# An attention and mixture-of-experts block: unfilled expert slots are skipped, weight tiles serve early reads, and TensorE's results join a partial sum

## The chip, the cores and the metric

The kernel runs on one core of one Trainium2 chip. The metric is the time of one execution on the device in microseconds. Before the change the median of six runs is 1692.75 us (1690.46 to 1701.3).

The core has five engines with a queue of instructions each: TensorE (PE, matrix multiplication; its weight loads are listed as PEld), VectorE (DVE), ScalarE (ACT), GpSimd (POOL) and SyncE (SP, which issues transfers here). Each works through its own queue in order and waits for the others through semaphores. The transfers (DMA) of all queues run on the same 16 DMA engines.

## The reference

T = 4096 tokens (16 sequences of 256) of width 256, in float32:

```python
x = x + layernorm(attention(layernorm(x)))     # 16 heads of 128, weights = codes * scales
h = layernorm(x)
scores = softmax(h @ gate.T)                   # 64 experts in 8 groups, the best 3 groups count
topk_w, topk_i = top 6 experts of each token
pos  = how many earlier (token, k) pairs chose the same expert
slot = expert * 96 + min(pos, 95)              # 96 slots an expert
buf[slot] = h[token]                           # a later token overwrites slot 95
out  = (silu(buf @ Wg.T) * (buf @ Wu.T)) @ Wd.T            # per expert, 96 rows
y    = sum over k of topk_w * out[slot]
x = x + layernorm(y + shared(h))               # shared: one gated layer of width 352
```

Most pairs of a crowded expert land in its last slot, so many tokens share that one row. An expert that few tokens chose leaves slots unfilled.

## The kernel before, in words

Three parts follow each other.

**Attention and routing (0 to about 1320 us).** A loop over 16 sequences x 16 heads runs as a software pipeline (project, scores, transpose, weigh; one head a step). A scheduler orders all queues but SP's first loads; the program can pin an instruction behind another on its engine (`issue_after`). Two sequences at a time, `route` finds the experts of 512 tokens and scatters their rows (token row, token number, weights) into `buf_d` with 24 indirect transfers on POOL (L584). In between, `check_codes` loads the weight codes again, piece by piece, and ORs their bits on DVE (L612), to see whether the codes fit the shorter format that this run assumes. `clear_slots` and `clear_sums` fill `buf_d` with a row that says "unfilled" (token number T + slot) and the sums with zero.

**Experts (about 1397 to 1588 us).** From here on the order of every queue is that of the program (`manual_schedule`). Experts come in groups of four. In the turn of expert e, PE transposes the rows of e + 2 (`bp`), multiplies those of e by Wg and Wu (`pg`), transposes the product of e - 1 (`ap`) and multiplies that of e - 2 by Wd (`eo`). ACT scales the result (`ob`), and POOL adds the 96 rows with an indirect, accumulating transfer (L885) to one of three sums in DRAM, `y0` to `y2`, at the rows' tokens. The sums take turns, so that neighbouring scatters don't wait for each other; `y2` takes none from expert 44 on. Rows of unfilled slots and of the last slots go to rows T to T + 95. The last slots' rows go into `ol` as well (L892, a transfer on ACT's queue, one a group); they reach their many tokens by a matmul later. Five groups of weights (`wg`, `wu`, `wd`, three tiles a group) are in SBUF; the next group's are loaded in the second turn of each group, after the next rows (`bn`, L828), all from SP. While the experts run, PE also computes pieces of the shared layer.

**Closing (about 1588 us to the end).** The output is made in eight chunks of 512 tokens, in the order `ends`: 0 to 3 (shared part already in y0), SG0 = 4 (shared part in SBUF, `ss`), and G = 5, G + 1, G + 2, whose shared part PE adds here. `pieces` says which parts of the shared layer PE computes between them (`shared_in`, followed by Silu on ACT and a product `aT` on DVE, `shared_act`). For chunk n the program issues: `put_out` (PE: last slots by `ovT` and `ol`, and the shared part, into a PSUM tile `ov`, of which there are two), the add of `ov` to the chunk's sum (DVE, L984), the statistics (DVE L991 and L992, ACT L994), the sum of the next chunk (`sum_y`: POOL y0 + y1, L969; DVE + y2, L970), and the normalization of chunk n (`norm_out`: DVE L1001 and L1003, ACT L1005, POOL + x L1006, output by SP L1007). y0, y1, y2 and `ovT` are loaded into tiles that take the place of the weights (L957, L959, L904).

Of the kernel before, what the change touches and what calls it, by code (L numbers as in the profile page):

```python
# [9 lines left out]
F32 = mybir.dt.float32  # L10
# [8 lines left out]
P = 128  # L19
# [31 lines left out]
def block_kernel(ctx, tc, x, wq, sq, wk, sk, wv, sv, wo, so, bqk, bv, bo, gateT, wg, wu, wd, sgT, suT, sdT, out):  # L51
# [10 lines left out]
    y_ds = [dram.tile([T + CAP, D], F32, name=f"y{i}_d") for i in range(NY)]  # L62
# [26 lines left out]
    def attention(split):  # L89
# [151 lines left out]
        def clear_sums(i):  # L241
            with tc.issue_after(marks[-1].ins):
                nc.vector.memset(zero, 0.0)
            r0 = 0 if i else SG0 * CG * P
            n = (T - r0) // P
            nc.sync.dma_start(
                y_ds[i][r0:T].rearrange("(p r) d -> p r d", p=P), zero.unsqueeze(1).to_broadcast([P, n, D])
            )
            nc.sync.dma_start(y_ds[i][T : T + CAP], zero[0:CAP, 0:D])
# [358 lines left out]
        def check_codes(n):  # L608

            todo = [(nm, j, i) for nm in views for j in range(NPC) for i in range(2)]  # L610
            if chks:
                nc.vector.tensor_tensor(bits, bits, chks.pop(), ALU.bitwise_or)  # L612
# [87 lines left out]
    def ffn(nm_, last_route, ph0):  # L700
# [72 lines left out]

        def load_group(g):
            w_g = ewp.tile([P, EG, DC, M], F32, tag="wg", name=f"wg{g}")
            nc.sync.dma_start(w_g, wg[:, g * EG : (g + 1) * EG])
            w_u = ewp.tile([P, EG, DC, M], F32, tag="wu", name=f"wu{g}")
            nc.sync.dma_start(w_u, wu[:, g * EG : (g + 1) * EG])
            w_d = ewp.tile([MH, EG, 2, D], F32, tag="wd", name=f"wd{g}")
            nc.sync.dma_start(w_d, wd[:, g * EG : (g + 1) * EG])  # L780
            wts[g] = (w_g, w_u, w_d)
# [94 lines left out]
        def expert_out(e):  # L876
# [5 lines left out]
            for mc in range(2):  # L882
# [6 lines left out]
                bounds_check=T + CAP - 1, oob_is_err=True, compute_op=ALU.add,  # L889
# [6 lines left out]
        ends = [0, G, 1, G + 1, 2, G + 2, 3, SG0]  # L896
        pieces = {0: [(G + 1, 1)], 1: [(G + 1, 2)], 2: [(G + 2, 0), (G + 2, 1)], 3: [(G + 2, 2)]}
        y2s = {}

        def load_y2(g):  # L900

            t = xp.tile([P, EG * RW], F32, tag="bn", name=f"y2_{g}", bufs=5)
            y2s[g] = t[:, 0 : CG * D].rearrange("p (c d) -> p c d", d=D)
            nc.sync.dma_start(y2s[g], y_ds[2][g * CG * P : (g + 1) * CG * P].rearrange("(c p) d -> p c d", p=P))  # L904

        with tc.manual_schedule():
# [7 lines left out]
            for e in range(E + 2):  # L914
# [11 lines left out]
                if e < E:  # L926
                    expert_mul(e, sg, pg)
                else:
                    if e > E:
                        shared_act(G, 0)  # L930
# [10 lines left out]
                if j == 1 and g >= 1:  # L941
                    if g + 3 < NG_:
                        load_buf(g + 3)
                    if g + EWB - 1 < NG_:
                        load_group(g + EWB - 1)
                    if g + 3 > NG_ and g < NG_:
                        load_y2(ends[g + 2 - NG_])

            ph3.close()
            yp = ph2.enter_context(tc.tile_pool(name="yp" + nm_, bufs=8, reuse_waits="tile"))  # L950
            loaded, stat = {}, {}

            def load_y(g):
                r = slice(g * CG * P, (g + 1) * CG * P)
                ys = [yp.tile([P, CG, D], F32, tag=f"y{i}", name=f"y{i}_{g}") for i in range(2)]
                for i in range(2):
                    nc.sync.dma_start(ys[i], y_ds[i][r].rearrange("(c p) d -> p c d", p=P))  # L957
                ovT = yp.tile([E, CG * P], F32, tag="ovT", name=f"ovT{g}")
                nc.sync.dma_start(ovT, ovT_d[:, r])  # L959
                if g not in y2s:  # L960
                    load_y2(g)
                loaded[g] = ovT, ys

            def sum_y(g, parts):

                ys = loaded[g][1]
                for c, n in parts:
                    r = slice(c, c + n)
                    nc.gpsimd.tensor_add(ys[0][:, r, :], ys[0][:, r, :], ys[1][:, r, :])  # L969
                    nc.vector.tensor_add(ys[0][:, r, :], ys[0][:, r, :], y2s[g][:, r, :])  # L970
                    if g == SG0:
                        nc.vector.tensor_add(ys[0][:, r, :], ys[0][:, r, :], ss[g][:, r, :])

            def put_out(g, c):

                ovT, y = loaded[g][0], loaded[g][1][0]
                po = ps.tile([P, 2, D], F32, tag="o", name=f"ov{g}_{c}")
                for i in range(2):
                    if g > SG0:
                        shared_out(po[:, i, :], g, c + i, True, False)  # L980
                    nc.tensor.matmul(  # L981
                        po[:, i, :], lhsT=ovT[:, (c + i) * P : (c + i + 1) * P], rhs=ol, start=g <= SG0, stop=True
                    )
                return lambda: nc.vector.tensor_tensor(y[:, c : c + 2, :], y[:, c : c + 2, :], po, ALU.add)  # L984

            def take_stats(g, c0, n):

                st = yp.tile([P, n, 6], F32, tag=f"st{n}", name=f"st{g}_{c0}", bufs=2)
                mv = yp.tile([P, n, 2], F32, tag=f"mv{n}", name=f"mv{g}_{c0}", bufs=2)
                for i in range(n):  # L990
                    nc.vector.bn_stats(st[:, i, :], loaded[g][1][0][:, c0 + i, :])  # L991
                    nc.vector.bn_aggr(mv[:, i, :], st[:, i, :])  # L992
                rs = yp.tile([P, n], F32, tag=f"rs{n}", name=f"rs{g}_{c0}", bufs=2)
                nc.scalar.activation(rs, mv[:, :, 1], AF.Sqrt, bias=eps_t)  # L994
                stat[g, c0] = rs, mv

            def norm_out(g, c0, n, eng):

                y = loaded[g][1][0][:, c0 : c0 + n, :]
                rs, mv = stat.pop((g, c0))  # L1000
                nc.vector.reciprocal(rs, rs)  # L1001
                nb = yp.tile([P, n], F32, tag=f"nb{n}", name=f"nb{g}_{c0}", bufs=2)
# [3 lines left out]
                eng.tensor_add(y, y, xs[:, g * CG + c0 : g * CG + c0 + n, :])  # L1006
                nc.sync.dma_start(out_v[:, g * CG + c0 : g * CG + c0 + n, :], y)  # L1007

            whole, halves = [(0, CG)], [(0, 2), (2, 2)]
            for g in ends[0:5]:  # L1010
                load_y(g)
# [5 lines left out]
            sum_y(ends[0], whole)  # L1017
            for n, g in enumerate(ends):
                last = n == len(ends) - 1
                nx = ends[n + 1] if not last else None  # L1020
                add = [put_out(g, 0), put_out(g, 2)]
                if n == 0:
                    shared_act(G + 1, 0)
                for u in pieces.get(n, []):
                    shared_in(*u)
                if last:
                    add[0]()
                    take_stats(g, 0, 2)
                    norm_out(g, 0, 2, nc.gpsimd)
                    add[1]()  # L1030
                    take_stats(g, 2, 2)
                    norm_out(g, 2, 2, nc.vector)
                    continue
                for f in add:
                    f()
                for u in pieces.get(n - 1, []):
                    shared_act(*u)
                take_stats(g, 0, CG)
                if n + 5 < len(ends):
                    load_y(ends[n + 5])  # L1040
                sum_y(nx, halves if n + 2 == len(ends) else whole)
                norm_out(g, 0, CG, nc.gpsimd)
            ph4.close()
            ph2.close()
# [48 lines left out]
```

## Time and profile before

| | |
|---|---|
| median of six runs | 1692.75 us |
| profiled execution | 1692.43 us |
| its span, first to last instruction | 1690.6 us |
| attention and routing, to 1320 us | PE busy 1142.9, DVE 961.9 us |
| rest of routing, first shared pieces, 1320 to 1397 | PE busy 71.9 of 77 us |
| experts, 1397 to 1588 | PE busy 183.1 of 191 us, DMA share 0.76 |
| closing, 1588 to 1690.6 | PE busy 68.6, DVE 47.8, POOL 36.8 of 102.6 us |

The profile is of one execution. "Busy" is time in which an engine ran an instruction. Idle time of an engine costs only where the end of the kernel waits for it, so it is read together with the chain of waits: followed back from the last instruction, at each step to what released it. A queue's name with a q (SPq, ACTq) means the issue of transfers. L12 is line 12 of the kernel.

### The profile page before, as it was taken

Reading aid. Unit: us, or ns where it says so; the run is one execution under the profiler, and the core shown is the slowest. Engines: PE = TensorE matmul, PEld = TensorE weight load, DVE = VectorE, ACT = ScalarE, POOL = GpSimd, SP = SyncE. Lnnn points to the kernel's source line nnn. Section 1 sums busy time; section 2 is a strip of 40 time slices with the busy share of each in tenths; the row PEclk is TensorE's granted clock in tenths of the full one; section 3 lists DMA queues with packets and bytes.
Section 4 is the critical chain, followed back from the end, with each engine's and each line's share of the span. In section 5 each row is a group of like instructions: output and inputs, shape, how many; then the busy total and the mean of one; then the engine's idle time right before and its main releaser. Section 6 shows DMA issues by size and latency. Waiting matters only on the chain.

```text
span 1690.6 us, 24626 instructions
## 1 busy us (share of the span) xinstructions
PE 1466.5 (87%) x8476; PEld 1237.7 (73%) x8476; DVE 1109.6 (66%) x3477; ACT 669.9 (40%) x1798; POOL 364.8 (22%) x333
## 2 busy tenths in 40 slices
PE   7999999599869968994999499959858999989894
PEld 5788898589768957894889498948757658868542
DVE  5879898488648855984798379838837614434344
ACT  4645554254335423542454245424424423223252
POOL 2410002300310040005000500140233034444443
PEclk9999999799979988998999799969979999999895
DMA  5364313410000000000000000000001676887781
GB/s 160 111 180 128 106 66 99 140 45 26 26 4 26 2 15 1 26 1 11 1 26 1 9 1 26 2 6 13 19 25 36 202 208 188 240 237 181 149 251 54
DMA packets 87175, 128.82 MB, mean 76 GB/s; under 512 B 12742, under 2 KB 69638, under 8 KB 85632
## 3 DMA queue, kind: packets, MB, share of 16 engines
q1 hardware_dynamic: 63024, 97.69, 19.3%
q0 software_dynamic: 18064, 17.82, 5.2%
q10 hardware_dynamic: 5952, 11.63, 2.1%
q8 instruction: 70, 1.15, 0.3%
q14 instruction: 65, 0.53, 0.1%
HBM read 81.98 MB, written 66.29 MB: 88 GB/s over the span
## 4 chain that ended last, share of the span: by engine, by line
PE 73%; another core or an unknown queue 9%; DVE 7%; DMA 3%; issue 3%; ACT 3%; POOL 1%; ACTq 0%; SPq 0%; POOLq 0%; DVEq 0%
PE po L353 12%; PE pq L308 12%; PE sc L320 11%; PE pt L342 7%; PE pp L372 6%; PE pv L293 6%; PE sp L736 4%; PE pg L857 4%; PE eo L883 3%; PE so L752 2%; PE ov L752 1%; ACT pe L328 1%; PE ov L981 1%; DMA wg<-wg 1%
## 5 line engine op out<-in xcount | busy, mean ns | idle before, releaser
L328 ACT ACTIVATE pe<-sc,nms 128x256 f32<-128x256 f32 x512 | 240.2, 475 | 217.3 <-DVE nms L324 156.1
L344 ACT COPY pT<-pt 128x512 f32<-128x512 f32 x256 | 150.3, 587 | 398.5 <-PE pt L342 251.1
L353 PE MATMUL po<-pT,v 128*128 128x256 f32 x1024 | 285.6, 392 | 17.1 <-DVE oT L357 11.6
L342 PE MATMUL pt<-ident,pe 128*128 128x128 f32 x1024 | 177.4, 285 | 141.2 <-DVE pe L334 102.7
L584 POOL DMA_INDIRECT buf_d<-h,si x192 | 189.3, 986 | 507.8 <-DVE si L581 428.7
L320 PE MATMUL sc<-qk 128*128 128x256 f32 x1024 | 274.0, 389 | 7.3 <-DVE qk L313 5.9
L342 PEld LDWEIGHTS pt<-ident,pe 128*128 128x128 f32 x1024 | 129.1, 144 | 188.1 <-issue 131.7
L313 DVE TENSOR_TENSOR qk<-pq,bqk_t 128x512 f32<-128x512 f32 x256 | 174.7, 682 | 107.0 <-remote 85.2
L308 PE MATMUL pq<-xnT,wq 128*128 128x256 f32 x1024 | 221.3, 332 | 0.6 <-DVE wq L191 0.4
L353 PEld LDWEIGHTS po<-pT,v 128*128 128x128 f32 x1024 | 181.1, 196 | 40.0 <-ACT pT L344 16.0
L355 DVE TENSOR_SCALAR oT<-po,bv_t 128x256 fp32r<-128x256 f32 x256 | 122.9, 480 | 117.4 <-PE po L353 53.4
L320 PEld LDWEIGHTS sc<-qk 128*128 128x128 f32 x1024 | 180.6, 195 | 25.8 <-DVE qk L313 5.7
L322 DVE TENSOR_REDUCE nm<-sc 128x2 f32<-128x512 f32 x256 | 175.1, 684 | 35.6 <-remote 16.9
L308 PE MATMUL pq<-xnT,wk 128*128 128x256 f32 x1024 | 177.0, 292 | 0.4 <-DVE wk L191 0.4
L308 PEld LDWEIGHTS pq<-xnT,wq 128*128 128x128 f32 x1024 | 162.3, 197 | 15.0 <-issue 1.5
L293 PE MATMUL pv<-wv,xnT 128*128 128x512 f32 x512 | 165.2, 444 | 2.7 <-POOL wv L195 2.5
L334 DVE TENSOR_SCALAR pe<-pe,rsum 128x256 f32<-128x256 f32 x512 | 164.7, 364 | 1.4
L308 PEld LDWEIGHTS pq<-xnT,wk 128*128 128x128 f32 x1024 | 146.5, 196 | 2.5 <-DVE wk L191 1.1
L372 PE MATMUL pp<-wo,oT 128*128 128x256 f32 x1024 | 136.1, 288 | 0.0
L372 PEld LDWEIGHTS pp<-wo,oT 128*128 128x128 f32 x1024 | 127.3, 191 | 1.0
L446 POOL DMA_DIRECT2D h_d<-h x9 | 7.4, 819 | 552.5 <-DVE h L441 275.6
L357 DVE SCALAR_TENSOR_TENSOR oT<-po,bv_t,oT 128x256 fp32r<-128x256 f32 x256 | 122.2, 477 | 2.7
(206 smaller groups left out, 1907.7 us busy)
## 6 DMA issues: line engine op xcount, KB each, us to landing
y<-y_d SPq DMA_DIRECT2D x24, 512.0 KB
wg<-wg SPq DMA_DIRECT2D x16, 704.0 KB
wu<-wu SPq DMA_DIRECT2D x16, 704.0 KB
wd<-wd SPq DMA_DIRECT2D x16, 704.0 KB
y_d<-zero SPq DMA_DIRECT2D x2, 4096.0 KB
buf_d<-empty SPq DMA_DIRECT2D x1, 6528.0 KB
bn<-buf_d SPq DMA_DIRECT2D x12, 408.0 KB
hs<-hT_d ACTq DMA_DIRECT2D x8, 512.0 KB
```

Source lines behind the costliest of these rows:

```text
L293: nc.tensor.matmul(pv, lhsT=x[:, dc, c * P : (c + 1) * P], rhs=ws["wv", j][:, dc, :], start=i == 0, stop=i == len(terms) - 1,)
L308: nc.tensor.matmul(pq[:, m, :], lhsT=w[:, dc, o : o + HD], rhs=x[:, dc, :], start=i == 0, stop=i == len(terms) - 1,)
L313: marks[0:] = [nc.vector.tensor_tensor(qk, pq, bqk_t[:, h, :].unsqueeze(2).to_broadcast([P, 2, S]), ALU.add)]
L320: nc.tensor.matmul(sc[:, c, :], lhsT=qk[:, 0, c * P : (c + 1) * P], rhs=qk[:, 1, :], start=True, stop=True)
L322: nc.vector.tensor_reduce(nm, sc, AX.X, ALU.max, negate=True)
L328: nc.scalar.activation(pe[:, c, :], sc[:, c, :], AF.Exp, bias=nms[:, c : c + 1], scale=SC, accum_out=ssum[:, c : c + 1])
L334: nc.vector.tensor_scalar_mul(pe[:, c, :], pe[:, c, :], rs[:, c : c + 1])
L342: nc.tensor.transpose(pt[:, kc, c * P : (c + 1) * P], pe[:, c, kc * P : (kc + 1) * P], ident)
L344: nc.scalar.copy(pT[b, h], pt)
L353: nc.tensor.matmul(po, lhsT=v[:, kc, o : o + HD], rhs=t[:, kc, :], start=kc == 0, stop=kc == 1)
L372: nc.tensor.matmul(pp, lhsT=x[:, h, c * P : (c + 1) * P], rhs=ws["wo", h // HPG][:, h % HPG, :], start=i == 0, stop=i == len(terms) - 1,)
L584: ins = nc.gpsimd.indirect_dma_start(out=buf_d[:, :], out_offset=bass.IndirectOffsetOnAxis(ap=si[:, c, k : k + 1], axis=0), in_=h[:, c, :] ...
```

## The change

1. **Unfilled rows.** `y0` to `y2` lose the 96 padding rows. A row whose number is T or more is outside the bound; the scatter now skips it in silence. The zero fill of the padding goes.
2. **Bit check.** The OR of `check_codes` is pinned behind the latest `qk` add, so that it stays in the step in which the program has it.
3. **One weight tile a group.** `wg`, `wu`, `wd` of a group are slices of one tile. A tile that has become free after the last groups is used for a chunk's y0, y1, y2 and `ovT`. `ovT` and y2 (finished at expert 41) are read in the turns 49, 53, 57, 61 and 65, where weights were loaded before; y0 and y1 after the last expert.
4. **Closing order.** `ov` is added to y2 as soon as PE has it. One step later follow y0 + y1 (POOL), + y2 (DVE) and the statistics, another step later the normalization. For chunk SG0, POOL adds the shared part to y2. SG0 and 3 swap places, and one piece of the shared layer comes a step earlier. The reads of the last three chunks wait for the output of the first three, whose tiles they get.

The core of the diff:

```diff
-    y_ds = [dram.tile([T + CAP, D], F32, name=f"y{i}_d") for i in range(NY)]
+    y_ds = [dram.tile([T, D], F32, name=f"y{i}_d") for i in range(NY)]
...
-            nc.sync.dma_start(y_ds[i][T : T + CAP], zero[0:CAP, 0:D])
...
             if chks:
-                nc.vector.tensor_tensor(bits, bits, chks.pop(), ALU.bitwise_or)
+                with tc.issue_after(marks[-1].ins):
+                    nc.vector.tensor_tensor(bits, bits, chks.pop(), ALU.bitwise_or)
...
+        def group_tile(name):
+            return ewp.tile([P, EG * (2 * DC * M + 2 * D)], F32, tag="w", name=name)
         def load_group(g):
-            w_g = ewp.tile([P, EG, DC, M], F32, tag="wg", name=f"wg{g}")
-            nc.sync.dma_start(w_g, wg[:, g * EG : (g + 1) * EG])
...
+            t = group_tile(f"w{g}")
+            n = EG * DC * M
+            w = [t[:, i * n : (i + 1) * n].rearrange("p (e c m) -> p e c m", e=EG, c=DC) for i in range(2)]
+            w.append(t[0:MH, 2 * n :].rearrange("p (e c d) -> p e c d", e=EG, c=2))
+            for a, b in zip(w, (wg, wu, wd)):
+                nc.sync.dma_start(a, b[:, g * EG : (g + 1) * EG])
...
-                bounds_check=T + CAP - 1, oob_is_err=True, compute_op=ALU.add,
+                bounds_check=T - 1, oob_is_err=False, compute_op=ALU.add,
...
-        ends = [0, G, 1, G + 1, 2, G + 2, 3, SG0]
-        pieces = {0: [(G + 1, 1)], 1: [(G + 1, 2)], 2: [(G + 2, 0), (G + 2, 1)], 3: [(G + 2, 2)]}
+        ends = [0, G, 1, G + 1, 2, G + 2, SG0, 3]
+        pieces = {0: [(G + 1, 1)], 1: [(G + 1, 2), (G + 2, 0)], 2: [(G + 2, 1)], 3: [(G + 2, 2)]}
...
+        def load_first(g):
+            t = group_tile(f"y{g}")
+            ys[g] = [t[:, i * CG * D : (i + 1) * CG * D].rearrange("p (c d) -> p c d", d=D) for i in range(NY)]
+            ovTs[g] = t[0:E, NY * CG * D : NY * CG * D + CG * P]
+            nc.sync.dma_start(ovTs[g], ovT_d[:, g * CG * P : (g + 1) * CG * P])
+            load_sum(g, 2)
...
                     if g + EWB - 1 < NG_:
                         load_group(g + EWB - 1)
-                    if g + 3 > NG_ and g < NG_:
-                        load_y2(ends[g + 2 - NG_])
+                    else:
+                        load_first(ends[g + EWB - 1 - NG_])
...
             def put_out(g, c):
-                ovT, y = loaded[g][0], loaded[g][1][0]
+                y = ys[g][2][:, c : c + 2, :]
...
+            def sum_y(g, c, n):
+                y = [t[:, c : c + n, :] for t in ys[g]]
+                nc.gpsimd.tensor_add(y[0], y[0], y[1])
+                if g == SG0:
+                    nc.gpsimd.tensor_add(y[2], y[2], ss[g][:, c : c + n, :])
+                nc.vector.tensor_add(y[0], y[0], y[2])
...
+            for i in range(n + 1):
+                if i < n:
+                    add = [put_out(ends[i], 0), put_out(ends[i], 2)]
+                    if i == 0:
+                        shared_act(G + 1, 0)
+                    for u in pieces.get(i, []):
+                        shared_in(*u)
+                    for f in add:
+                        f()
+                    for u in pieces.get(i - 1, []):
+                        shared_act(*u)
+                if i == n:
+                    break
+                if i:
+                    g = ends[i - 1]
+                    sum_y(g, 0, CG)
+                    take_stats(g, 0, CG)
+                if i > 1:
+                    norm_out(ends[i - 2], 0, CG, nc.gpsimd)
+                    if i - 2 + EWB < n:
+                        load_first(ends[i - 2 + EWB])
+                        load_rest(ends[i - 2 + EWB])
+            g = ends[-1]
+            sum_y(g, 0, 2)
+            take_stats(g, 0, 2)
+            norm_out(ends[-2], 0, CG, nc.gpsimd)
+            sum_y(g, 2, 2)
+            norm_out(g, 0, 2, nc.gpsimd)
+            take_stats(g, 2, 2)
+            norm_out(g, 2, 2, nc.vector)
```

## The prediction

> **What bounds the kernel now.** I read the page first, then the busy times by stage, the chain of waits over the expert part and the closing part, the waits of SP's queue, and the timeline of the closing part. The page and the stages:
>
> ```profile
> span 1690.6 us, 24626 instructions
> PE 1466.5 (87%) x8476; PEld 1237.7 (73%) x8476; DVE 1109.6 (66%) x3477; ACT 669.9 (40%) x1798; POOL 364.8 (22%) x333
> ```
>
> ```profile
> 1397.00:1588.00 191.00, 183.14 (x1102) 152.51 (x1101) 74.10 (x261) 54.01 (x136) 90.88 (x64) 0.98 0.76 193
> 1588.00:1690.60 102.60, 68.64 (x187) 37.69 (x185) 47.84 (x117) 34.87 (x57) 36.79 (x18) 0.75 0.60 172
> ```
>
> In a stage row the numbers are length, then busy time of PE, PEld, DVE, ACT and POOL. Up to 1588 PE is busy 183 of 191 us: only its stalls can be won there. In the closing 102.6 us no engine is full (PE 68.6, DVE 47.8, POOL 36.8): that stretch is made of waits. The chain of waits shows PE's stalls in the expert part, and SP's waits show what lies behind them:
>
> ```profile
> 1471.08 5.07 DMA wg<-wg
> ...
> 1496.21 9.06 DMA wg<-wg
> 1505.34 0.58 ACTq L892
> ```
>
> ```profile
> SPq L828 <- DMA y_d<-ob,bn: 113.5, 16, 10.9
> ```
>
> ACT issues a small transfer (`ol`, L892) once per group; it can go only when a weight load has landed, and the Silu that PE's next expert needs stands behind it in ACT's queue. The weight loads stand behind `bn` loads on SP, which wait 113.5 us in total for scatters. So late scatters make late weights make a blocked ACT: 5.07 + 9.06 = 14.1 us, and some 2 us more at half clock (the pg/eo matmuls after 1506 take about twice as long).
>
> In the closing part the timeline of all engines shows a ring:
>
> ```profile
> 1640.04 1.23 DVE L970 TENSOR_TENSOR y<-y,y 128x1024 f32<-128x1024 f32 x1
> 1641.18 0.17 DVE L1001 RECIPROCAL rs<-rs 128x4 f32<-128x4 f32 x1
> 1641.38 0.16 DVE L1003 SCALAR_TENSOR_TENSOR nb<-mv,rs 128x4 f32<-128x4 f32 x1
> ...
> 1641.58 2.08 ACT L1005 ACTIVATE y<-y,nb,rs 128x256 f32<-128x256 f32 x4 [1.14 <-DVE nb L1003]
> ...
> 1643.73 2.34 POOL L1006 TENSOR_TENSOR y<-y,xs 128x1024 f32<-128x1024 f32 x1 [7.94 <-ACT y L1005]
> ...
> 1646.03 2.34 POOL L969 TENSOR_TENSOR y<-y,y 128x1024 f32<-128x1024 f32 x1
> ...
> 1648.41 1.23 DVE L970 TENSOR_TENSOR y<-y,y 128x1024 f32<-128x1024 f32 x1
> ```
>
> POOL's queue is in program order, so its sum for a later chunk (L969) stands behind the residual add of an earlier one (L1006). That add waits for ACT's normalization, which waits for DVE's `nb`, which in DVE's queue follows the sum that waits for POOL. From start to start: sum 1.14, `rs` and `nb` 0.40, ACT 2.15, POOL 2.30 + 2.38 = 8.37 us, exactly 1640.04 to 1648.41. The statistics (L991, L992) aren't in it: here they run on DVE while ACT and POOL are at work.
>
> **The change part by part.** Times below are in the clock of this trace.
>
> Skipped rows. The reference's routing on its inputs leaves 21 of 64 experts under 96 tokens; with the last slot of each, 1146 of 6144 rows (19%) are not scattered. That a skipped row costs no packet shows in the scatter of L584: 192 instructions of 128 rows are 24576 rows, but POOL's queue has 18064 packets in all. POOL's own 1.43 us a scatter stay. The scatters of j=2 and 3 of a group sit on the loop scatter, `bn`, weights (its period is 12.6 us: `bn` at 1458.07, 1470.65, 1483.34). Of those that gate the weights behind the 9.06 us stall (experts up to 27) the empty rows make 2.8 full scatters (experts 10, 19, 22, 23); scatters follow each other at 2 to 3 us in such a burst, so SP gains about 7 us there. The deleted padding DMAs (3 x 96 KB, issued far from any wait) are worth 0.
>
> One weight tile instead of three. The load of a group now waits until the group's last `eo` has run, not its last `pg`: the first refill moves from 1405.39 to where wd goes now, 1411.81, with wu, wd and the next `bn` behind it on SP. Later ones wait for `bn` anyway. Cost to the loop: 0 to 6.4 us; I take 3. Net, SP is 4 us early at the 9 us stall, and PE leaves the expert part x = 4 us early. Bounds: -4 (no gain from rows, refill late) to +16 (all stalls go).
>
> The `bits` ORs move from 97 to 390 us to steps 88 to 216, some 430 to 1050 us: 33 x 0.68 = 22.4 us of DVE. There PE is busy 69.6 of 70 us in the even batches and DVE 57.8, so four ORs a batch (2.7 us) fit in 12 us of idle DVE: 0. If that cover is gone it is the 22.4 us. The DVE waits on their loads now (L612, 9.4 us) lie in a stretch where 16 steps take the same 70 us as without them, so nothing is won either. Range: -2 to +4.
>
> Early reads. `ovT` and y2 of four chunks now arrive during the expert part and the fifth's right after it, so PE's 5.6 us wait for `ovT` at 1592.33 goes: PE runs on. On SP they stand behind the last `bn` and weights and ahead of the y0/y1 reads, so nothing urgent is queued behind them. They add 2 x 0.64 MB and 2 x 0.13 MB to two y2 reads that are there now, each of which stretched a scatter by about 1 us: the scatters may end 2 us later, but the first y0/y1 sums aren't what is late (below). Chunks 5 to 7 get the tiles of chunks 0 to 2, so SP holds their reads until that chunk's output has been written: for chunk 5 by about 1628, with `ovT` there at 1631 and PE asking for it at 1638. Hidden by 7 us; if it is later, PE waits the rest.
>
> The closing order. Now chunk i's `ov` is added to y2, and only one step later come POOL's y0+y1, DVE's sum, the statistics of that sum; then `nb` of the chunk before. So DVE's 2.14 us of statistics (four pairs, 1602.58 to 1604.72) enter the ring between sum and `rs`: 8.37 + 2.14 = 10.5 us a chunk, whatever PE does. What is late next is that ring. Step by step, with PE free at 1592.3 - x: `ov` of an unshared chunk 1.9, of a shared one 8.3, a piece of `shared_in` 3.6 (chain rows of L981, L752, L736).
> - The sum of chunk 1 stands on DVE behind the `ov` adds of chunk 2: 1592.3 + 1.9 + 3.6 + 8.3 + 7.1 + 1.9 = 1615.1, adds and two `aT` 2.0: 1617.1. (Before: 1604.72.)
> - Sum 2 is PE's: 1.3 for a PSUM buffer, 3.6 + 8.3 of PE, 1.4 of DVE: 1629.7. Sums 3, 4, 5 by the ring: 1640.2, 1650.7, 1661.2. Sum 6 carries the shared part on POOL, 2.3 more: 1674.0. (Before, sum 6 is at 1662.92.)
> - Tail: 8.1 to POOL's first half of the last chunk, 1.3 to its sum, 6.5 through statistics, chunk 6's `nb`, ACT and POOL to the second half, then 1.3 + 1.0 + 1.0 + 0.8 + 1.1 + 0.7 to the last add: 1695.8. From the last add's end to the span's end it is now 1683.2 to 1690.6, 7.4: 1703.2 - x.
> - PE idles some 4.5 us before the last shared chunk (its `aT` waits in ACT's queue behind a normalization). In this trace 3.0 us of idle (1643.3 to 1646.3) was followed by a granted clock of 0.50 from 1646 to 1658, where 20 of these 24 matmuls and the 8 with `ol` took 14.3 us. So that chunk may take 16.6 in place of 8.3, and the end is 1708 - x.
>
> The Trainium skill, "TensorE: Matmul & The Clock Gate", Part 1, says that about 3.4 us of sustained work brings the clock back. By it the chunk would take about 10 us, the ring would stay the bound, and the slow case would fall away. This trace differs: the clock stayed at half for 12 us of unbroken matmuls.
>
> I take the middle of 1703.2 and 1708: 1705.5 - 4 = 1701.5, against 1690.6. The profiled execution took 1692.43, 1.8 more than its span and 0.3 under the median 1692.75: **1703 us**.
>
> **The rivals.**
> - Expert stalls vanish (x = 15). The completion semaphore that L892 shares with a weight load depends on the order of the DMAs, which the single tile shifts; against it, order and number in a group stay the same. 1705.5 - 15 + 1.8 = 1692: no change.
> - Faster: the ring does not hold, because sum, normalization and residual add of neighbouring chunks overlap. Then PE decides, with 52.3 us of closing work (1.9 x 5 + 8.3 x 3 + 3.6 x 5): 1644.6, plus 1.3 for the adds and 20 from the last chunk's first sum to the end, minus x: 1662, or 1664 in time. It decides from the point where a ring step is under PE's 6.5 us a chunk. Against it: the 8.37 above closes to the last digit with queues in order.
> - Rows and tiles win nothing (x = -4): 1711.
> - The ORs are exposed: 1703 + 22 = 1725. For it, only that PE is full there.
>
> **How the numbers follow.** A measurement tells about 0.3% (5 us) from no change: 1687.7 to 1697.8. Forecast 0.50, with its own range 1696 to 1710; vanishing stalls 0.20; nothing won 0.13; faster ring 0.08; exposed ORs 0.09. Faster is the faster ring and a little of the vanishing stalls, 0.11; no change is most of that rival and the forecast's low end, 0.27; slower 0.62. Leaving out the faster ring, the exposed ORs and some edge, the range is 1688 to 1712.
>
> **What would show it.** Right: L970's successor starts 10.5 us apart in the later closing steps, with statistics between sum and `nb`; the second sum near 1613; no wait for `ovT`; the last POOL sums 10 us later than now; `bn` loads under 12.6 us apart around experts 20 to 27. Wrong: ring steps of 8 us or less, POOL's sums not waiting behind L1006's add, attention's 70 us batches longer by more than 1 us, or the two expert stalls gone.

## The result and the profile after

The changed kernel takes 1704.98 us (median of 20 runs, 1699.03 to 1710.33) where the kernel before took 1693.36 in the same comparison (46 runs): ratio 1.0062, 95% interval 1.005 to 1.0074, slower by 0.6%. The forecast was 1703. The profiled execution took 1702.36 us. Its page begins:

```profile
span 1700.5 us, 24626 instructions
PE 1457.4 (86%) x8476; PEld 1233.2 (73%) x8476; DVE 1105.8 (65%) x3475; ACT 666.1 (39%) x1796; POOL 366.7 (22%) x334
```

The same stages (length, then busy time of PE, PEld, DVE, ACT, POOL, then the granted clock, the DMA share and GB/s):

```profile
1397.00:1588.00 191.00, 184.34 (x1089) 151.23 (x1088) 73.46 (x256) 53.90 (x136) 85.92 (x61) 0.98 0.76 199
1588.00:1700.50 112.50, 56.84 (x176) 32.15 (x174) 44.32 (x114) 30.65 (x53) 44.31 (x22) 0.74 0.43 134
```

PE is busy for less time in the closing stretch than before, and the stretch is longer: it is made of waits, more than before. A cleaner cut is by the Silu of the experts. The first is at 1396.6 (before 1400.7), the last at 1571.05 (1575.7). So attention and routing are 4.1 us shorter, the expert part 0.5 us, and the closing part, from the last Silu to the end of the span, grows from 114.9 to 129.5: +14.6. Together that is +9.9 us of span.

In the expert part the chain of waits (start, us, what) no longer has the two stalls of before, but others of the same make:

```profile
1484.56 13.25 DMA w<-wd
1497.88 0.61 ACTq L896
...
1512.26 12.22 DMA y_d<-ob,bn
1524.68 3.94 DMA bn<-buf_d
1528.70 0.59 ACTq L896
```

ACT's small transfer `ol` (L896 now) still waits, here until a load of weights (`wd`) and a load of rows (`bn`) have landed. In the trace each of the two loads has the completion semaphore that `ol` uses next, and ACT waits for it first. SP's wait for scatters ahead of `bn` (total, times, longest) is no shorter than the 113.5 us of before:

```profile
SPq L832 <- DMA y_d<-ob,bn: 119.6, 16, 12.8
```

The skipped rows are seen in POOL's DMA queue. First before, then after: packets, MB, share:

```profile
q0 software_dynamic: 18064, 17.82, 5.2%
```

```profile
q0 software_dynamic: 18064, 16.66, 4.8%
```

The packets are as many, only the bytes fall. In the trace 1146 packets of the experts' scatters now have 8 bytes and take 11 ns each on average, and the other 4998 have 1024 bytes and take 127 ns (125 before).

A piece of the closing ring, from the timeline of all engines (DVE sum L982, `nb` L1001; ACT square root L992, normalization L1003):

```profile
1636.18 1.22 DVE L982 TENSOR_TENSOR y<-y 128x1024 f32<-128x1024 f32 x1 [2.12 <-POOL y L979]
...
1639.75 1.28 ACT L992 ACT_TABLE_LOAD   x1 [6.41 <-DVE rs L999]
1639.76 0.16 DVE L1001 SCALAR_TENSOR_TENSOR nb<-mv,rs 128x4 f32<-128x4 f32 x1
...
1641.04 0.30 ACT L992 ACTIVATE rs<-mv,eps_t 128x4 f32<-128x4 f32 x1
1641.25 2.06 ACT L1003 ACTIVATE y<-y,nb,rs 128x256 f32<-128x256 f32 x4
```

Between the sum at 1636.18 and `nb` at 1639.76 stand the statistics, as forecast. What was not forecast is the table load: ACT computed a Silu before, so the square root for the next chunk (L992), which stands ahead of the normalization in ACT's queue, first loads its table. From sum to sum this step takes 11.88 us (1636.18 to 1648.06); the next, with no Silu in it, takes 10.59 (to 1658.65), where the forecast had 10.5.

Where in the closing part the 14.6 us arise is seen in DVE's second and seventh sum, called sum 1 and sum 6. First before, then after:

```profile
1604.72 1.23 DVE L970 TENSOR_TENSOR y<-y,y 128x1024 f32<-128x1024 f32 x1
...
1662.92 1.21 DVE L970 TENSOR_TENSOR y<-y,y 128x1024 f32<-128x1024 f32 x1
```

```profile
1612.31 1.21 DVE L982 TENSOR_TENSOR y<-y 128x1024 f32<-128x1024 f32 x1
...
1671.54 1.23 DVE L982 TENSOR_TENSOR y<-y 128x1024 f32<-128x1024 f32 x1 [7.85 <-POOL y L981]
```

From the last Silu to sum 1 it is 41.3 us, before 29.0: +12.2. From sum 1 to sum 6 it is 59.2, before 58.2: +1.0. From there to the end it is 29.0, before 27.7: +1.4. So most of the loss is there before the ring turns, because sum 1 now stands behind PE's work for chunk 2 (counted in the order of `ends`). The new order would have to win it back afterwards, since PE is then further ahead, and it does not.

### The profile page after: what moved, and what is told of

It is laid out like the page before. It is cut to its first block, busy times and chain, and to the rows that moved or that the text cites. A ratio compares the mean times of both kernels' runs of the same rounds, so it can differ in the third digit from the quotient of the medians.

```text
span 1700.5 us, 24626 instructions
## 1 busy us (share of the span) xinstructions
PE 1457.4 (86%) x8476; PEld 1233.2 (73%) x8476; DVE 1105.8 (65%) x3475; ACT 666.1 (39%) x1796; POOL 366.7 (22%) x334
## 4 chain that ended last, share of the span: by engine, by line
PE 65%; another core or an unknown queue 9%; DMA 8%; DVE 7%; issue 6%; ACT 2%; POOL 2%; SPq 0%; ACTq 0%; POOLq 0%; DVEq 0%
PE po L352 12%; PE pq L307 12%; PE sc L319 11%; PE pp L371 7%; PE pt L341 6%; PE pv L292 6%; DMA y_d<-ob,bn 5%; PE sp L736 2%; PE pg L861 2%; PE eo L887 2%; PE so L752 1%; DVE qk L312 1%; DVE pe L333 1%; ACT pe L327 1%
## 5 line engine op out<-in xcount | busy, mean ns | idle before, releaser
L352 PEld LDWEIGHTS po<-pT,v 128*128 128x128 f32 x1024 | 180.3, 196 | 39.2 <-issue 13.4
```

The lines of the kernel that those rows point to most:

```text
L352: nc.tensor.matmul(po, lhsT=v[:, kc, o : o + HD], rhs=t[:, kc, :], start=kc == 0, stop=kc == 1)
```

## The experiments

In some sessions attention ran without the eight stalls of some 20 us that the traces before and after have: the kernel before then takes 1512 us instead of 1677 to 1693. So each ratio below is to the kernel before in the same session, and across sessions only the lengths of the expert part (first to last Silu) and of the closing part (last Silu to the end) are compared, which the stalls don't touch. The times are medians; the ratio is worked out from all runs and need not be the quotient of the two medians. The closing part is read from one execution each; where only rows or ORs differ from the kernel before it varies from 114.7 to 117.8, and the changed kernel has 129.5 and 130.4, so differences of 3 us say nothing.

| kernel | before, same session, us | this, us | ratio (95%) | closing part, us |
|---|---|---|---|---|
| before (first profile) | | | | 114.9 |
| changed (first comparison) | 1693.36 | 1704.98 | 1.0062 (1.005 to 1.0074) | 129.5 |
| changed again | 1677.51 | 1687.0 | 1.0072 (1.0045 to 1.0099) | 130.4 |
| before + skipped rows | 1511.8 | 1508.5 | 0.9999 (0.9973 to 1.0025) | 114.7 |
| before + pinned ORs | 1511.8 | 1497.46 | 0.9914 (0.9886 to 0.9942) | 117.8 |
| before + one tile | 1677.51 | 1681.03 | 1.0013 (0.9992 to 1.0034) | 123.2 |
| changed, late reads | 1677.51 | 1697.73 | 1.0107 (1.0074 to 1.0141) | 142.7 |
| changed, old order | 1511.77 | 1509.84 | 0.9978 (0.9954 to 1.0002) | 129.7 |
| changed, statistics last | 1511.8 | 1502.12 | 0.9933 (0.991 to 0.9956) | 122.8 |
| changed, POOL ahead | 1511.8 | 1497.69 | 0.9915 (0.9882 to 0.9947) | 115.9 |
| changed, reordered | 1677.51 | 1665.12 | 0.9933 (0.9908 to 0.9958) | 105.9 |
| reordered, adds first | 1511.77 | 1496.03 | 0.9879 (0.9831 to 0.9926) | 109.8 |
| adds first, six `bn` tiles | 1511.77 | 1499.79 | 0.9926 (0.9901 to 0.995) | 110.3 |
| reordered, Silu first | 1511.88 | 1483.18 | 0.9805 (0.9784 to 0.9826) | 101.7 |

**The change again.**

> The changed kernel itself once more, beside the kernel before on the same chip. On the chip of the first experiments the whole kernel takes about 1512 us, since the eight stalls of some 20 us in attention are absent, and the pinned ORs alone win 13 us there. If attention wins 13 us in the changed kernel as well and the closing part loses 14.6 (last Silu of the experts to the end: 129.5 us, before 114.9), the two cancel: ratio 0.997 to 1.003, some 1510. If the ORs' gain does not carry over: ratio 1.006 to 1.010. If this chip is one with the stalls: 1705 against 1693, as in the first comparison.

The ratio is 1.0072, the first result once more, again with the stalls. What the changed kernel takes without them wasn't run.

**Skipped rows alone.**

```diff
-    y_ds = [dram.tile([T + CAP, D], F32, name=f"y{i}_d") for i in range(NY)]
+    y_ds = [dram.tile([T, D], F32, name=f"y{i}_d") for i in range(NY)]
...
-            nc.sync.dma_start(y_ds[i][T : T + CAP], zero[0:CAP, 0:D])
...
-                bounds_check=T + CAP - 1, oob_is_err=True, compute_op=ALU.add,
+                bounds_check=T - 1, oob_is_err=False, compute_op=ALU.add,
```

> The kernel before with the skipped rows alone (sums of T rows, rows beyond the bound skipped, no padding cleared). The prediction's step: SP is 7 us early at the 9 us stall of expert 38, the bn loads come under 12.6 us apart, and some 4 to 7 us are won: about 1687 to 1689 where the kernel before has 1693. Rival, from the changed kernel's profile, in which bn loads are 12.5 to 14.8 us apart although 19% of the rows are gone: a scatter's time in the loop is its issue and its way there and back, not its rows; within 2 us of the kernel before.

The ratio is 0.9999: the rival came. The `bn` loads come 11.6 to 13.2 us apart, as with the pinned ORs alone, where all rows are moved (12.0 to 13.4). A scatter has 18 skipped rows on average, 18 x 0.115 us on 16 engines = 0.13 us, and it takes 3.2 to 10.7 us from issue to landing (median 8.6).

**Pinned ORs alone.**

```diff
-                nc.vector.tensor_tensor(bits, bits, chks.pop(), ALU.bitwise_or)
+                with tc.issue_after(marks[-1].ins):
+                    nc.vector.tensor_tensor(bits, bits, chks.pop(), ALU.bitwise_or)
```

> The kernel before with the ORs of the bit check pinned to their steps, and nothing else. The prediction's step: hidden, 0 (-2 to +4). From the changed kernel's profile, whose attention ends 4 us earlier (first Silu of the experts at 1396.6 and not 1400.7): if the pinned ORs are the cause, about 4 us faster, 1689 where the kernel before has 1693, with the first Silu near 1397. If not, no change, and the 4 us came from another part or from one execution to the next.

The ratio is 0.9914: faster by 0.9% alone, and the first Silu of the experts comes at 1202.9, against 1216.0 in the kernel with the skipped rows, whose attention is that of the kernel before. Of these 13.1 us 12.0 lie in the four batches (of 16 steps each) in which the ORs were before: from the first `sc` of the first to the first `sc` after the fourth 283.2 us there (98.9 to 382.1), 271.2 here (99.1 to 370.3). DVE's waits in that stretch of the kernel with the skipped rows, which the pinned ORs don't have (total, times, longest):

```profile
DVE bits L611 <- DMA chkwv<-wv: 7.2, 5, 5.5
...
DVE bits L611 <- DMA chkwk<-wk: 4.1, 6, 1.2
...
DVE bits L611 <- DMA chkwo<-wo: 2.8, 3, 1.7
```

The scheduler had drawn the ORs so far forward that 15 of the 32 wait for their loads, 14.3 us in all, and DVE's queue stands behind them; in the same stretch PE lost 4.5 us in one wait for an `oT`. Pinned to the step in which the program has them, they find the loads done. In the first comparison the same four batches are only 3.3 us shorter (299.9 and 296.6), and the ORs' waits in the trace before are 9.4 us. That the stalls hide part of the waits there is likely, but not shown.

**One tile alone.** The diff is the tile part of the change (`group_tile`, `load_group`) in the kernel before.

> The kernel before with one weight tile a group, and nothing else. The prediction's step: the refills wait for the last eo and not the last pg, 0 to 6.4 us on the loop, 3 taken: ratio 1.000 to 1.004. In the changed kernel's profile the last scatter ends 27.4 us after the last Silu of the experts (before: 14.4); if the single tile makes the scatters late, it is over 20 us here, and the closing part starts later by as much; if the early reads do, it stays under 18.

The ratio is 1.0013, and the last scatter ends 23.0 us after the last Silu (before 14.4; with the pinned ORs 18.0). The first refill starts 11.1 us after the first Silu, not 4.7 (the kernel with the pinned ORs), the `bn` load behind it at 22.6, not 19.0. The loop of scatter, `bn` and weights, 12.7 us a group, never makes up for it. PE doesn't feel it among the experts (173.6 us from first to last Silu, 173.5 with three tiles), but at the end: it now waits 13.0 us for `ovT`, which stands on SP behind the reads that wait for the scatters:

```profile
PE ov L985 <- DMA ovT<-ovT_d: 13.0, 1, 13.0
```

**Late reads.**

```diff
-                    else:
-                        load_first(ends[g + EWB - 1 - NG_])
...
             for g in ends[0:EWB]:
+                load_first(g)
                 load_rest(g)
```

> The changed kernel with the reads of ovT and y2 of the first five chunks issued after the last expert, ahead of each chunk's y0 and y1, rather than during the experts. Theory A: the early reads (3.9 MB between the last weights and the last scatters) delay the scatters by some 10 us; without them the last scatter ends about 17 us after the last Silu and not 27, the first sum in the closing part comes 4 to 8 us earlier, but PE waits about 5 us for ovT as in the kernel before; in sum 0 to 5 us faster than the changed kernel. Theory B: the scatters are late from the single tile on; then they stay at 27, and the reads that come later cost 3 to 8 us.

Half of either theory came, and neither one's number. The early reads do delay the scatters, by 5 us (22.4 us after the last Silu without them, 27.6 with them), but they are worth 12.3 us of the closing part all the same (130.4 against 142.7): without them PE waits 4.5 us for `ovT`, works at half clock for the next 17.1 us (1584.23 to 1601.29), and sum 1 comes 53.9 us after the last Silu, not 41.5.

**Old closing order in the changed kernel.** The closing loop, `ends`, `pieces` and `sum_y` of the kernel before, on the new tiles with the early reads.

> The changed kernel with the closing order of the kernel before (ov added after y0 + y1 + y2, statistics at once, sum of the next chunk, normalization; old order of chunks and pieces), while rows, ORs, tile and early reads stay as changed. It prices the order by itself. If the ring with the statistics in it is what costs (the prediction's step): the closing part, from the last Silu of the experts to the end, is 115 to 120 us and not 130, ratio 0.995 to 1.000 to the kernel before. Rival: the scatters, 27 us behind the last Silu, are what costs (the kernel before with one tile has 23 us and a closing part of 123 us): then 124 to 132 us, since the old order can't use PE's results before the y0 and y1 sums, and the ratio stays at 1.004 or over.

The closing part is 129.7 us: the rival came. The ratio, 0.9978, is under the rival's 1.004, likely because it was run without the stalls, and without them the ORs win 0.9%. In the old order `ov` is added to y0 + y1 + y2, so PE waits for the late scatters (columns as before: total, times, longest):

```profile
PE ov L752 <- DVE y L974: 17.7, 2, 17.1
```

The new order has no such wait (its longest in the closing part is 6.5 us, for the DVE add). It saves that and pays it back, with a sum 1 that stands behind PE's work for chunk 2 and then ring steps of 10.6 to 11.9 us. That both orders come out at 129.5 to 130.4 us is a coincidence of two different limits.

**Statistics last.** In each step the normalization of chunk i - 2 goes ahead of the statistics of chunk i - 1.

```diff
                 if i:
-                    g = ends[i - 1]
-                    sum_y(g, 0, CG)
-                    take_stats(g, 0, CG)
+                    sum_y(ends[i - 1], 0, CG)
                 if i > 1:
                     norm_out(ends[i - 2], 0, CG, nc.gpsimd)
...
+                if i:
+                    take_stats(ends[i - 1], 0, CG)
```

> The changed kernel with one reorder: in each closing step the normalization of chunk i - 2 is issued ahead of the statistics of chunk i - 1, so on DVE `nb` follows the sum directly. Ring theory: the ring of sum, nb, ACT, POOL + x, POOL y0 + y1 loses the 2.14 us of statistics, a ring step falls from 10.6 (1648.06 to 1658.65 in the changed kernel's profile) to about 8.4; four to five steps follow one another in the ring, so the end is 8.6 to 10.7 us earlier: 1694 to 1697 where the changed kernel has 1705. Rival: PE's shared chunks, half clock or the reads set the 11.9 us steps; then it moves by less than 3 us (1702 to 1706).

The timeline of the ring:

```profile
1456.92 1.22 DVE L982 TENSOR_TENSOR y<-y 128x1024 f32<-128x1024 f32 x1
...
1458.46 2.07 ACT L1003 ACTIVATE y<-y,nb,rs 128x256 f32<-128x256 f32 x4 [9.04 <-DVE nb L1001]
...
1460.61 2.34 POOL L1004 TENSOR_TENSOR y<-y,xs 128x1024 f32<-128x1024 f32 x1 [8.16 <-ACT y L1003]
...
1465.29 1.23 DVE L982 TENSOR_TENSOR y<-y 128x1024 f32<-128x1024 f32 x1 [3.45 <-POOL y L979]
```

1456.92 to 1465.29 is 8.37 us, the step of the kernel before to the last digit; another is 8.37 too (1435.74 to 1444.11). Statistics and table load are out of the ring. The closing part is only 6.7 us shorter, not 8.6 to 10.7: the step to sum 2 is PE's own (13.7 us; 12.0 in the changed kernel), and in the step to sum 4 (12.8 us) a shared chunk's second `ov` came 7.5 us after the first, not 4.2, at half clock.

**POOL ahead.** y0 + y1 of chunk i is issued one step earlier, ahead of the residual add of chunk i - 2.

> The changed kernel with POOL's y0 + y1 of chunk i issued one step earlier, ahead of the residual add of chunk i - 2 (for chunk SG0 the shared part is added to y0 rather than to y2; same work). Ring theory: the ring then closes only over two steps, (8.4 + 2.1) / 2 = 5.3 us a chunk, and no longer binds; PE (52.3 us of closing work, 6.5 a chunk) or DVE (per chunk two adds of ov 2.0, sum 1.1, statistics 2.1, nb 0.4, aT 0.7: 6.3) decides. First sum at about 1605 as now, eight steps of 6.3 to 6.5, then 20 us of tail and output: 1672 to 1680 in time. Rival: late scatters, reads of chunks 5 to 7 that wait for the outputs of 0 to 2, or a PE at half clock keep the steps near 10: 1695 to 1705.

The closing part takes 115.9 us, 13.6 less than in the changed kernel and not the 25 to 33 expected. The ring no longer binds, and what comes next is PE's wait for `aT` (4.3 us, behind a normalization on ACT) with the half clock after it: the longest step from sum to sum, 14.7 us, holds both.

**Reordered, three versions.** All have POOL ahead, and Silu and `aT` of a piece in the step in which PE computes it. The first has the normalization of chunk i - 2 ahead of the adds of `ov`:

```diff
+                for c in (0,) if i < n - 1 else (0, 2):
+                    sum_first(ends[i], c, CG if i < n - 1 else 2)
+                for u in pieces.get(i, []):
+                    shared_in(*u)
                 if i > 1:
                     norm_out(ends[i - 2], 0, CG, nc.gpsimd)
...
+                for f in add:
+                    f()
+                if i:
+                    sum_y(ends[i - 1], 0, CG)
+                for u in pieces.get(i, []):
+                    shared_act(*u)
+                if i:
+                    take_stats(ends[i - 1], 0, CG)
```

> The changed kernel with another closing order, same work (the shared part of chunk SG0 is added to y0): POOL's y0 + y1 one step ahead, the normalization of chunk i - 2 at the beginning of step i, Silu and aT of a piece in the step in which PE computes it, statistics last. Ring theory: no ring is left; Silu no longer stands behind a normalization, so PE does not idle and keeps its clock. From the last expert's Silu PE needs 17 us to the closing part, 52 us in it, and 20 to 25 us follow: 90 to 97 us, where the changed kernel has 129.5, the first reorder 122.8, the POOL-ahead one 115.9 and the kernel before 114.9: 30 us faster than the changed kernel, 1.5 to 2% faster than the kernel before. Rival: late scatters and reads of y0, y1 hold DVE and with it PE; then 105 to 115 us and no more than the POOL-ahead order.

The closing part takes 105.9 us: in the range of the rival, though 10 us better than the POOL-ahead order, and 0.7% faster than the kernel before. But neither scatters nor reads held PE at the place that cost most. `sum_first` is POOL's y0 + y1. PE on the timeline:

```profile
1603.53 1.99 PE L971 MATMUL ov<-ol,y 64*128 64x256 f32 x8
1609.43 2.93 PE L752 MATMUL ov<-sd_t,aT 128*128 128x256 f32 x6 [3.91 <-DVE y L974]
...
1617.35 1.56 PE L752 MATMUL ov<-sd_t,aT 128*128 128x256 f32 x6
```

After one wait of 3.9 us the same six matmuls take 2.93 us, not 1.56, until 7.9 us of unbroken work have passed. In the second version the adds go ahead of the normalization, and `aT` goes behind the statistics:

> The reordered closing part once more, with the adds of ov ahead of the normalization on DVE and aT behind the statistics. In the reordered run PE waited 3.9 us for an add that stood behind aT and nb, and ran at half clock for the next 12 us (a shared chunk in 11.5 us, not 8.3, and two more ov at half speed). If that wait made the half clock, both go: the closing part takes 95 to 100 us (105.9 in the reordered run), ratio about 0.988. Rival: the clock falls for another reason or DVE is now the bound: 104 to 108 us, no change against the reordered run.

There was no gain (109.8, over the rival's range too): the statistics went ahead of Silu too, so on ACT the square root, and its table, went ahead of Silu; `aT` came later, and PE again waited 3.8 us at the same place. In the last version Silu is ahead of the square root on ACT, and the statistics ahead of `aT` on DVE:

> The reordered closing part a third time, with Silu ahead of the square root on ACT and the statistics ahead of aT on DVE (same work). In the two other versions PE waited 3.9 and 3.8 us before chunk G + 2 for an add that stood on DVE behind aT, and aT behind a Silu; the chunk then ran at half clock. If that one wait is taken away (Silu comes when PE has the piece, aT behind 3.3 us of sum and statistics), PE runs on: chunk G + 2 in 8.3 us and not 11.5, the closing part (last Silu of the experts to the end) 95 to 101 us where those had 105.9 and 109.8 and the changed kernel 129.5; ratio to the kernel before 0.982 to 0.988. Rival: DVE, held by the first sum until the scatters and reads are done, is the bound whatever PE does: 104 us or more, ratio 0.988 to 0.994.

```profile
1433.63 1.99 PE L974 MATMUL ov<-ol,y 64*128 64x256 f32 x8
1436.49 1.56 PE L755 MATMUL ov<-sd_t,aT 128*128 128x256 f32 x6 [0.86 <-DVE y L977]
```

The wait is 0.86 us, the six matmuls take 1.56, and the closing part 101.7, just over the expected 95 to 101: 1483.18 us against 1511.88, 2% faster than the kernel before (some 0.9% of it are the ORs', by the run with them alone) and the fastest of all. Sum 1 is as late as in the changed kernel, 42.7 us after the last Silu, but from sum 1 to sum 6 it takes 37.1 us, not 59.2. What is late now is PE's wait of 6.2 us for the `ovT` of the last chunk, whose tile comes free only with an output.

**Six tiles of rows.** Beside the adds-first version, `bn` has six tiles; the Silu buffer of the shared layer and the experts' product have one each.

> As the adds-first kernel, with six tiles of expert rows (bn) where there are five; to make room the Silu buffer of the shared layer and the experts' product have one tile and not two. It takes SP's wait for scatters (119.6 us in the changed kernel, 12.7 us a group) out of the way of the weights without touching the scatters. Loop theory (the prediction's): weights come some 12 us earlier, ACT's ol transfers no longer wait for them, and the expert part (first to last Silu 175.3 us in the changed kernel) falls to 163 to 168; 6 to 11 us faster than the adds-first kernel. Rival: the scatters themselves set the pace through the ob tiles, or the single buffers cost as much: 173 us or more.

The rival came: the expert part takes 178.2 us, where the adds-first version has 171.7 and the runs with the changed kernel's expert part have 170.3 to 175.6. SP's wait for scatters falls (114.0 us in the adds-first version), but ACT now waits for them, since the scaled rows `ob` need tiles that the scatters free; the adds-first version has no such wait of ACT:

```profile
SPq L832 <- DMA y_d<-ob,bn: 86.2, 14, 11.5
```

```profile
ACT ob L888 <- DMA y_d<-ob,bn: 22.8, 4, 7.8
```

The other half of the rival, that the two single buffers cost as much, was not tried apart: DVE's waits for Silu ahead of the product grew too (17.2 us, 8.2 in the adds-first version).

## Why the prediction was right, and where it was not

The number was right (1703 against 1705), and so were the path of the closing part and its bound, the ring. That it was right to 2 us is luck in part: two pairs of errors cancelled, one in front of the closing part (under x = 4) and one in it (under half clock). The forecast's sums with x = 4 against the trace, where all but the last row follow its fast case, without half clock (which ends at 1699.2), and the last row is the middle that it took:

| | forecast | measured |
|---|---|---|
| sum 1 | 1613.1 | 1612.31 |
| sum 2 | 1625.7 | 1624.33 |
| sum 3 | 1636.2 | 1636.18 |
| sum 4 | 1646.7 | 1648.06 |
| sum 5 | 1657.2 | 1658.65 |
| sum 6 | 1670.0 | 1671.54 |
| last add, its end | 1691.8 | 1694.42 |
| end of span | 1701.5 | 1700.5 |

- **The ring**: right, with one term missed. The table load and the square root stand in it where a Silu went before: two steps of 11.9 us (to sums 3 and 4), +1.3 us each. Taking the statistics and the table load out gave back 8.37 exactly. The trace puts two of POOL's waits in the ring down to reads of y, but the normalization ended less than 0.1 us before POOL's add in these steps as in the others, so the reads did not set the pace.
- **Skipped rows, 7 us for SP**: wrong. The count of packets was read as "a skipped row costs no packet"; in these scatters it still makes one, of 8 bytes, and a whole row is worth only 0.127 us of one of 16 engines. The count of L584 could not have shown it: by their sizes (16, 1100, 2184, 3268 and 4352 bytes, which are four rows of 1088 bytes or of 4), its packets carry four rows each, 6144 for 24576 rows, and a skipped row counts 4 bytes in them. The 2 to 3 us between scatters are issue and waiting, not rows. Measured alone, the ratio is 0.9999.
- **x = 4**: PE left the expert part 4.7 us early, but 4.1 of these are attention's, 3.3 in the four batches that lost their ORs, which the forecast had at 0 with -2 as its lower end. Two errors of one size cancelled: the rows' gain that did not come, and the ORs' that was not foreseen.
- **The ORs**: the step that failed is "nothing is won either". The forecast saw the 9.4 us in which DVE waits for their loads and set them aside, since the batches looked equally long. They were not (69.7 and 68.6 us for the 16 steps from 165), and without the stalls the waits cost 12 us. The ORs themselves (32 of 0.68 us in the trace, where the forecast counted 33) are hidden, as forecast.
- **One tile, 3 us on the loop**: the delay has the right size (the first refill is 6.4 us late), but the wrong place. PE's experts did not feel it. With the tile alone the scatters ended 8.6 us later after the last Silu than in the kernel before, and the closing part was 8.3 us longer (5.0 and 5.4 against the kernel with the pinned ORs).
- **Early reads**: PE's wait for `ovT` went, as forecast. "The scatters may end 2 us later" became 5, on top of the tile's. "The first y0/y1 sums aren't what is late" held: before the adds of chunk 2 DVE waited 0.83 us for PE, and the sum of chunk 1 followed them. In the old order it did not hold (17.1 us of PE waiting).
- **The order itself** was forecast as the loss, and in the changed kernel it is: sum 1 was forecast 12.4 us later than before by the trace's clock (8.4 with x = 4) and came 7.6 later, and the ring kept the order from winning that back. The runs with a weaker ring win back a part, nearly all, and more than all of it, with scatters and a sum 1 just as late (closing part 122.8 with statistics last, 115.9 with POOL ahead, 101.7 with Silu first, 114.9 before). What the forecast did not see is that the old order on the same tiles would have lost as much, 129.7 us, for another reason, the scatters that end late. How the new order does with scatters as early as before was not run; by the trace its sum 1 waits for PE (0.83 us), not for them.
- **Half clock**: PE waited 4.3 us for `aT` (forecast 4.5), and the matmuls ran at half speed from 1634.12 to 1639.22, 5.1 us, less than the 12 of the trace before; the ring stayed the bound. So of the forecast's two cases the fast one came, and its middle was 2.4 us too high at this place. The two table loads, 2.6 us that it did not have, filled the gap: that is the second pair. In the second profile of the same kernel the same wait of 4.26 us was followed by 13.2 us at half clock (1615.82 to 1629.05), and the ring step there took 12.4 us, not 11.9. The Trainium skill, "TensorE: Matmul & The Clock Gate", Part 1, says that about 3.4 us of sustained work brings the clock back. Here it was back after 4.0 us of work in the shortest case (statistics last, after a wait of 1.2) and after 17.1 in the longest (late reads, after 4.5), so no single figure tells which case comes.
- **The stalls by `ol`**: the rival "expert stalls vanish" did not come. It also had less to win than it said: the 14.1 us are the length of the DMAs in the chain, while PE itself waited 7.9 us in the whole expert part before, and 6.7 after. The six `bn` tiles show that a simple cure fails: where SP waits less for the scatters, ACT waits for them at `ob`.

## What to carry to other kernels

Where engines hand work round in program order, write down the ring with every instruction that stands between two of its members, table loads too; a step that is only moved may enter it. A transfer that ends late is not felt where it is late but at the first reader that has nothing else to do: look which order can use the time until then, and put what PE's next chunk needs (here Silu, `aT`, the add) ahead of what only the output needs. When a number comes out right, check its terms one by one: here two pairs of wrong ones cancelled. Rows left out of a scatter save bytes; first see whether bytes are what the scatter's time is made of.

## What the runs showed of the hardware

- A row that an accumulating indirect scatter skips still makes a packet: 1146 packets of 8 bytes, 11 ns each, in place of 1024 bytes at 127 ns. In the plain indirect scatter of L584 a packet carries four rows, and a skipped one counts 4 bytes in it.
- PE's wait of 3.9 us cost about as much again afterwards: for 7.9 us matmuls took 2.93 us per six instead of 1.56, so the same work took 3.7 us longer. With a wait of 0.86 us at the same place there was none of it. How long PE had to work until the full clock was back varied from 4.0 to 17.1 us, and between two profiles of one kernel, after the same wait of 4.26 us, from 5.1 to 13.2.
- The stalls of attention are not the program's alone. The kernel before takes 1677 to 1693 us in some sessions and 1512 us in others, and one chip, number 4, shows both. The odd batches, in which POOL scatters, take some 92 us with the stalls, and 66 to 70 without (kernel with the skipped rows). What holds PE there stays open.
- DVE's waits for small loads, 9.4 us, cost 3.3 us in a session with the stalls, and 14.3 us of them cost 12.0 in one without. That a stall elsewhere covers part of such waits fits this, but is not shown.
- An activation table load took 1.28 us, and the next activation began 1.30 us after its start. Where it stood between two members of the ring, the step from sum to sum was 11.9 us and not 10.6.
